# First front of a four-image hybrid network: two channel groups convolved on VectorE, first scan parts moved within the chip, edge count and scatters placed elsewhere

## The chip, the cores and the metric

The kernel runs on one core of one Trainium2 chip. The metric is the device time of one execution in microseconds; the time of the kernel before is the median of three runs. The profile is a further execution, recorded by the hardware profiler.

## What is computed

The input is four images of 32 x 32 pixels with 256 channels. Four layers follow: layer 0 (below), a bottleneck convolution with a residual, a graph attention over 1024 tokens with a mask made from a list of edges and a mixture of experts, and a second state-space layer with another mixture of experts. The first front belongs to layer 0:

```python
x = _layernorm(src, ln1_g, ln1_b)
x = x @ w_in + b_in                                   # 256 -> Dn = 512 channels
x = conv_general_dilated(x, conv_w, (1, 1), 'SAME', feature_group_count=Dn) + conv_b   # 3x3, depthwise
x = jax.nn.gelu(x)
proj = x @ w_x
dt_raw, Bm, Cm = jnp.split(proj, [R, R + N], axis=-1) # R = 16, N = 64
dt = jax.nn.softplus(dt_raw @ w_dt + dt_bias)
A = -jnp.exp(A_log)
def step(h, inp):
    xt, dtt, Bt, Ct = inp
    h = jnp.exp(dtt[:, :, None] * A) * h + (dtt * xt)[:, :, None] * Bt[:, None, :]
    return h, jnp.einsum('bdn,bn->bd', h, Ct)
```

The mask of the attention is `zeros((N, N)).at[src, dst].set(True)`.

## The kernel before, in words

**Scans and stages.** One generator, `scans` (line 366), runs all eight state-space scans (four images, layers 0 and 3) as 1280 scan units of 128 partitions x 1024 steps. It is the metronome of the kernel. For one unit, SP loads a decay tile (`load`, line 432: 512 KB, broadcast from the `dt` array in memory), ScalarE takes its exponential (`decay`), TensorE spreads a row of "parts" over the states (`first`: `ps_rep`), VectorE multiplies by B and runs `tensor_tensor_scan`, GpSimd multiplies by C (`h`), and TensorE sums over the states (`pair`: `ps_y`). Decay tiles have five buffers, `h` tiles five. `load` runs four units ahead.

Everything else is a *stage*: `front` (layer 0 up to the scan's inputs), `middle` (the end of layer 0 up to the scan inputs of layer 3), `last`. Stages are generators, too. `run` (562) advances the current stage between two half-units as long as the planned clocks of the engines (`Metered.COST`, a table of prices) are not ahead of VectorE's. So each engine's instructions stand in one fixed order, set by these prices at build time. Before the first unit can run, `need` (527) advances the first front until its first parts are ready: this is the prologue.

**The first front** (`front`, 711, with b = 0). The normalised image is transposed (`turned`), and for each of four groups of 128 channels (`DC` = 4) TensorE projects two halves of 512 pixels (`ps_in`), ScalarE writes them into a padded tile `pad` (34 x 34), ScalarE makes nine diagonal matrices of the taps (`diag`), and TensorE convolves: for each half nine fp32 matmuls of 128 x 512 with a diagonal matrix as weights (`ps_cv`). ScalarE applies the gelu and writes `u`. Then `ps_x` gives the 16 rows `dtr` and the B and C rows `bct`.

**The softplus items** (`steps`, 591). For each (group, half) TensorE makes `ps_dt`, ScalarE the pieces of the softplus, then dt (`sp_r`) and dt times u are formed, and the product is split into three bf16 parts (`parts`). In the first front the first two items are done by VectorE ahead of the others. SP stores dt (line 635) and parts (650) in memory; `chunk` (387) loads the B and C rows (401) and the parts, three loads of 32 partitions x 4 x 1024 (408), as the tile `S`, ahead of the units that use it; the pieces of S are addressed by j, 0 to 3, 32 channels each: the first 16 units use j = 0 and 1.

**The mask's work** is a third generator, `mask_work` (`setup`, 1846): tables for the scans (`scan_setup`, 323), then `mask_prepare` (1008): load the edges, transpose them (`ps_e`), make a linear index, count the edges of each row (`cnt`, `ps_c`), sort by eight rounds of `largest` (1089), switch on the count for rounds beyond 64 edges, and write the indices `where`. Then `scatter` (1112): 64 indirect DMAs by GpSimd that write zeros into a mask of 4 MB in memory, four switches for more columns, and one copy of the mask to bf16. `need` advances this generator once for each step of the front, `run` once for each unit.

**The vectors** (biases, gains, taps) are loaded by `load_vectors` (198) before all else: 27 small loads in two packs, each pack transposed by TensorE.

Of the kernel before, what the change touches and what calls it, by code (L numbers as in the profile page):

```python
# [16 lines left out]
P = 128  # L17
NB = 4
L = 1024
# [34 lines left out]
        ("L0_conv_conv_b", 4), ("L0_conv_dt_bias", 4), ("L0_conv_D_skip", 4), ("L0_conv_ln2_g", 4),  # L54
        ("L0_conv_ln2_b", 4), ("L1_conv_b1", 1), ("L1_conv_g1", 1), ("L1_conv_be1", 1),
        ("L1_conv_m1", 1), ("L1_conv_v1", 1), ("L1_conv_b2", 1), ("L1_conv_g2", 1),
        ("L1_conv_be2", 1), ("L1_conv_m2", 1), ("L1_conv_v2", 1), ("L2_attn_bq", 2),
        ("L2_attn_bk", 2), ("L2_attn_bv", 2), ("L3_attn_b_in", 8), ("L3_attn_b_conv", 4), ("L3_attn_b_dt", 4),
    ),
    (("L2_ffn_b1", 16), ("L3_ffn_b1", 32)),  # L60
)

# [70 lines left out]
class Hybrid:  # L133
    def __init__(self, ctx, tc, a, out):
        self.ctx, self.tc, self.nc, self.a = ctx, tc, tc.nc, a
        self.out = out.rearrange("b h w c -> (b h w) c")
        nc = self.nc
        self.const = const = ctx.enter_context(tc.tile_pool(name="const", bufs=1))
        self.dram = ctx.enter_context(tc.tile_pool(name="dram", bufs=1, space=DRAM))

        self.ident = const.tile([P, P], F32, name="ident")
        make_identity(nc, self.ident)
        self.identb = const.tile([P, P], BF16, name="identb")
        nc.vector.tensor_copy(self.identb, self.ident)

        order = const.tile([P, NEXP], I32, name="order")
        nc.gpsimd.iota(order, pattern=[[-1, NEXP]], base=NEXP, channel_multiplier=0)
        self.order = const.tile([P, NEXP], F32, name="orderf")
        nc.vector.tensor_copy(self.order, order)
        self.eps = {}  # L150
        for e in (1e-5, 1e-3):
            self.eps[e] = const.tile([P, 1], F32, name=f"eps{len(self.eps)}")
            nc.vector.memset(self.eps[e], e)

        self.x0 = const.tile([P, TB, C], F32, name="x0")
        nc.sync.dma_start(self.x0, self.image(a["x"].rearrange("b h w c -> (b h w) c"), 0))
        self.w_in0 = self.weight(const, "L0_conv_w_in", 2)
        for _ in self.norm(const, self.x0, TB, self.x0, "ln0"):
            pass

        self.blocks = const.tile([P, P], F32, name="blocks")
        make_block_diagonal(nc, self.blocks, 4)
        self.states = {0: 64, 3: 16}
        E = mybir.EngineType
        self.sides = (E.PE, E.DVE, E.Activation, E.SP)
        self.mem = {}
# [31 lines left out]
    def load_vectors(self):  # L198

        nc, a = self.nc, self.a  # L200
        self.vec = {}
        with self.tc.tile_pool(name="vstage", bufs=1) as sp, self.tc.tile_pool(
            name="vpsum", bufs=1, space=PSUM
        ) as pp:
            for n, pack in enumerate(VEC_PACKS):
                rows = sum(k for _, k in pack)
                stage = sp.tile([rows, P], F32, name=f"vstage{n}")
                r = 0
                for name, k in pack:
                    src = a[name]  # L210
                    if name == "L0_conv_conv_w":
                        src = src.rearrange("i j u (k p) -> (i j u k) p", p=P)
                    elif len(src.shape) == 2:
                        src = src.rearrange("e (k p) -> (e k) p", p=P)
                    else:
                        src = src.rearrange("(k p) -> k p", p=P)
                    nc.sync.dma_start(stage[r : r + k, :], src)
                    r += k
                ps = pp.tile([P, rows], F32, name=f"vps{n}")
                nc.tensor.transpose(ps, stage, self.ident[:rows, :rows])  # L220
                cols = self.const.tile([P, rows], F32, name=f"cols{n}")
                nc.vector.tensor_copy(cols, ps)
                r = 0
                for name, k in pack:
                    self.vec[name] = cols[:, r : r + k]
                    r += k
# [96 lines left out]
    def scan_setup(self, stage, name, n):  # L323
# [8 lines left out]
        flat = self.a[name].rearrange("(u g) n -> u (g n)", g=G)  # L332
        for k in range(0, units, P):
            m = min(P, units - k)
            raw = stage.tile([m, P], F32, name=f"Ar{k}_" + name)
            nc.sync.dma_start(raw, flat[k : k + m, :])
            turned = stage.tile([m, P], F32, name=f"At{k}_" + name)
# [23 lines left out]
        return cols, spread, collect  # L361
# [4 lines left out]
    def scans(self, mp, psum):  # L366
# [19 lines left out]

        def chunk(k):
# [6 lines left out]
            n = self.states[scan[0]]  # L394
            self.need(scan, d)
            if d == 0:
                bct = self.mem["bc", *scan]
                pair = []
                for t in range(2):
                    x = mp.tile([P, L], F32, tag=f"rows{t}", name=f"rows{t}", bufs=2)  # L400
                    nc.sync.dma_start(
                        x, bct[t * n : (t + 1) * n, :].unsqueeze(1).to_broadcast([n, P // n, L])
                    )
                    pair.append(x)
                rows[scan] = pair
            S = mp.tile([3 * 32, 4, L], BF16, tag="S", name="S", bufs=2)
            for s in range(3):
                nc.sync.dma_start(
                    S[32 * s : 32 * s + 32, :, :],
                    self.mem["parts", *scan, d][s].rearrange("(j p) t -> p j t", p=32),  # L410
                )
# [84 lines left out]

        for k in range(AHEAD):
            chunk(k)
        for k in range(4):
            load(k)  # L500
# [26 lines left out]
    def need(self, scan, d):  # L527

        late = False
        while ("parts", *scan, d) not in self.ready:  # L530
# [3 lines left out]
            for _ in range(SCATTERED if self.sorted else 1):  # L534
                next(self.mask_work, None)
        if late:

            self.clock.update(dict.fromkeys(self.clock, max(self.clock.values())))
# [23 lines left out]
    def run(self):  # L562
# [3 lines left out]
        self.alone = False  # L566
        nc, tc = self.nc, self.tc
        with tc.tile_pool(name="scan", bufs=1) as mp, tc.tile_pool(
            name="scps", bufs=1, space=PSUM
        ) as psum, tc.tile_pool(name="sdps", bufs=1, space=PSUM) as side, tc.manual_schedule():  # L570
            self.side_psum(side)
            self.mask_work, self.sorted = self.setup(), False
            clock = self.clock = dict.fromkeys(Metered.COST, 0.0)
            self.nc = Metered(nc, clock)
            for n, _ in enumerate(self.scans(mp, psum)):
                if n % 2:
                    next(self.mask_work, None)
                now = clock["vector"]
# [12 lines left out]
    def steps(self, fp, key, w, src, chunks, bias, u, between=None):  # L591
# [65 lines left out]
        if between is not None:  # L657
# [6 lines left out]
            yield from between  # L664
            for item in ahead:
                add(item, nc.vector)
            for item in ahead:
                split(item)
            for item in ahead:
                low(item, nc.vector)  # L670
            for item in ahead:
                store(item)
# [38 lines left out]
    def front(self, b):  # L711
# [3 lines left out]
        with tc.tile_pool(name=f"f{b}", bufs=1, side="right") as op:  # L715
# [4 lines left out]
            with tc.tile_pool(name=f"fa{b}", bufs=1, side="right") as fp:  # L720
# [8 lines left out]
                pads = [fp.tile([P, 34, 34], F32, name=f"pad{i}") for i in range(2)]  # L729
                for i in range(2):  # L730
                    nc.gpsimd.memset(pads[i], 0.0)
# [4 lines left out]
                yield from self.turned(x, TB, xT, (vec["L0_conv_ln1_g"], vec["L0_conv_ln1_b"]))  # L736
                got = {}

                def inward(item):
                    d, g, k = item  # L740
                    pad = pads[d % 2]
                    if g < 0:
# [10 lines left out]
                        )  # L753
                        if h == 0:
# [32 lines left out]
                items = []  # L787
                for d in range(DC):
                    items += [(d, -1, 0), (d, -1, 1)]
                    items += [(d, g, k) for g in range(2) for k in range(3)]  # L790
                yield from self.pipe(items, inward, cost=2.3)
            with tc.tile_pool(name=f"fb{b}", bufs=1, side="right") as fp:
# [215 lines left out]
    def mask_prepare(self):  # L1008
# [16 lines left out]
        with tc.tile_pool(name="mprep", bufs=1) as mp:  # L1025
# [15 lines left out]
            yield from [None] * 8  # L1041
# [6 lines left out]
            yield from [None] * 4  # L1048
            for a, rawf in enumerate(rawfs):
# [5 lines left out]
                yield  # L1055
# [21 lines left out]
            ps = self.early("ps_c")  # L1077
            nc.tensor.transpose(ps[:1, :P], cnt, self.ident)
            top = mp.tile([1, 1], F32, name="top")
            nc.vector.tensor_reduce(top, ps[:1, :P], AX.X, ALU.max)  # L1080
            more = mp.tile([1, len(SCATTERS)], F32, name="more")
            for i, (first, _) in enumerate(SCATTERS):
                nc.vector.tensor_scalar(more[:, i : i + 1], top, float(first), None, ALU.is_gt)
            nc.vector.tensor_copy(self.more, more)
            order = mp.tile([P, ne], F32, name="sorted")
            few = SCATTERS[0][1]
            nc.vector.memset(order[:, few:], 0.0)
# [9 lines left out]
            yield  # L1097
# [7 lines left out]
            yield  # L1105
# [3 lines left out]
        self.sorted = True  # L1109
# [66 lines left out]
    def attention(self, b, tb):  # L1176
        nc, tc, vec = self.nc, self.tc, self.vec
        with tc.tile_pool(name=f"at{b}", bufs=1, side="right") as op:
# [9 lines left out]
            with tc.tile_pool(name=f"aa{b}", bufs=1, side="right") as fp:  # L1188
# [25 lines left out]
                yield from self.large_scores(fp, qT, kT, large)  # L1214
                nc.sync.dma_start(maskT, self.mem[("maskT",)].rearrange("j p f -> p j f"))
# [630 lines left out]
    def setup(self):  # L1846
        with self.tc.tile_pool(name="prep", bufs=1) as st:
            yield
            self.tables = {}
            for scan, name, n in ((0, "L0_conv_A_log", 64), (3, "L3_attn_A_log", 16)):  # L1850
                self.tables[scan] = self.scan_setup(st, name, n)
                yield
        yield from self.mask_prepare()
# [35 lines left out]
def hybrid_kernel(tc, a, out):  # L1889
    with ExitStack() as ctx:  # L1890
        k = Hybrid(ctx, tc, a, out)
        k.load_vectors()
# [38 lines left out]
```

## Time and profile before

| | |
|---|---|
| median of three runs (lowest to highest) | 6504.83 us (6499.96 to 6507.34) |
| the profiled execution's own time | 6499.29 us |
| its span in the profile | 6497.3 us |
| mean granted TensorE clock | 0.831 |
| busy: TensorE, VectorE, ScalarE, GpSimd | 5253.9, 5119.6, 3415.4, 3646.8 us |
| first scan unit on VectorE starts at | 152.56 us |
| scan unit 256 starts its scan at | 1240.3 us |

How to read it: times of the timelines are in us from the span's start. A row shows its start, how long it took, the engine, the line, the operation with output and input tiles, and in brackets the idle time of the engine before it with what ended it. Nearly all operations carry the line of one helper (L124), so groups are told apart by the names of their tiles. In the rows of the stretches of time the columns are: stretch and its length, then the busy time (and number of instructions) of TensorE's matmuls, its weight loads, VectorE, ScalarE and GpSimd, then the granted TensorE clock, the busy share of the DMA engines and GB/s. A matmul of fp32 counts as two records.

### The profile page before, as it was taken

How to read it: one execution, taken by the hardware profiler on the slowest of the kernel's cores; microseconds unless marked ns; L12 is line 12 of the kernel's file. 1: busy time of each engine (PE TensorE's matmuls, PEld its weight loads, DVE VectorE, ACT ScalarE, POOL GpSimd, SP SyncE). 2: the span in 40 equal slices, each digit the busy share in tenths (PEclk: the TensorE clock that was granted, in tenths of full speed). 3: DMA queues.
4: the chain of work that ended last, by engine and by line, in shares of the span. 5: the costliest groups of instructions: out<-in, count | busy, mean ns of one | idle time of the engine just before them, and what ended most of it. 6: DMA issues, size and time to landing. Idle time of an engine off the chain costs nothing. (4 is left out here: it accounts for less than half of the span.)

```text
span 6497.3 us, 59722 instructions
## 1 busy us (share of the span) xinstructions
PE 5253.9 (81%) x20235; PEld 2124.1 (33%) x20320; DVE 5119.6 (79%) x4310; ACT 3415.4 (53%) x4095; POOL 3646.8 (56%) x1793
## 2 busy tenths in 40 slices
PE   6667868689797569979689679798699688978979
PEld 2022212222342022234145232252255222524656
DVE  3978988988898998889889988898899981258311
ACT  3346656355576335567568445577387354246311
POOL 2957677765557666555856665556756661055200
PEclk9577868689898569979789789898699689878989
DMA  2454554643355566335635664345544750156221
GB/s 101 145 163 159 180 163 160 198 150 124 119 174 170 180 169 164 113 128 184 195 132 176 195 159 135 112 146 178 182 164 163 196 148 15 46 147 166 68 67 34
DMA packets 348077, 936.58 MB, mean 144 GB/s; under 512 B 37140, under 2 KB 119648, under 8 KB 346144
## 3 DMA queue, kind: packets, MB, share of 16 engines
q1 hardware_dynamic: 345616, 930.35, 46.0%
q0 software_dynamic: 2128, 2.13, 0.2%
q8 instruction: 168, 2.75, 0.2%
q14 instruction: 165, 1.35, 0.1%
HBM read 842.59 MB, written 93.95 MB: 144 GB/s over the span
## 5 line engine op out<-in xcount | busy, mean ns | idle before, releaser
L124 POOL TENSOR_TENSOR h<-h,rows 128x1024 f32<-128x1024 f32 x1280 | 3033.0, 2372 | 1835.8 <-DVE h L124 1572.9
L124 DVE TENSOR_TENSOR_SCAN h<-dA,ps_rep 128x1024 f32<-128x1024 f32 x1280 | 2923.7, 2284 | 131.4 <-ACT dA L124 3.1
L124 DVE TENSOR_TENSOR ps_rep<-ps_rep,rows 128x1024 f32<-128x1024 f32 x1280 | 1551.7, 1212 | 188.5 <-PE ps_rep L124 183.9
L124 ACT ACTIVATE dA<-dA,A_L_conv_A_log 128x1024 f32<-128x1024 f32 x1024 | 1147.7, 1144 | 612.1 <-DMA dA<-dt 547.2
L124 PE MATMUL ps_rep<-S,spread_L_conv_A_log 96*128 96x512 bf16 x2048 | 763.2, 463 | 767.6 <-DVE h L124 716.2
L124 PE MATMUL ps_y<-h,collect_L_conv_A_log 128*32 128x512 f32 x4096 | 775.8, 767 | 61.5 <-POOL h L124 61.0
L124 PE MATMUL ps_h<-xTm,we 128*128 128x512 f32 x1536 | 714.2, 604 | 0.0
L124 PE MATMUL ps_e<-we,h_m 128*128 128x256 f32 x3072 | 700.4, 380 | 2.3 <-ACT h_m L124 2.3
L124 PEld LDWEIGHTS <-spread_L_conv_A_log 96*128 96x128 bf16 x2048 | 159.9, 103 | 1568.9 <-DVE h L124 1236.1
L124 ACT ACT_TABLE_LOAD x483 | 619.7, 1283 | 59.4 <-PE ps_h L124 44.1
L124 PEld LDWEIGHTS ps_e<-we,h_m 128*128 128x128 f32 x3072 | 579.4, 190 | 152.5 <-issue 61.1
L124 DVE SCALAR_TENSOR_TENSOR tb<-ps_e,cw,tb 128x256 f32<-128x256 f32 x512 | 219.9, 474 | 409.3 <-PE ps_e L124 409.2
L124 ACT ACTIVATE h_m<-ps_h,cols 128x512 f32<-128x512 f32 x384 | 260.2, 687 | 501.4 <-PE ps_h L124 498.9
L124 ACT ACTIVATE p<-ps_sc 128x512 f32<-128x512 f32 x432 | 234.5, 594 | 386.0 <-PE ps_sc L124 255.4
L124 PEld LDWEIGHTS ps_h<-xTm,we 128*128 128x128 f32 x1536 | 291.9, 193 | 331.7 <-issue 286.9
L124 ACT ACTIVATE dA<-dA,A_L_attn_A_log 128x1024 f32<-128x1024 f32 x256 | 290.6, 1146 | 200.0 <-DMA dA<-dt 172.3
L124 PE MATMUL ps_rep<-S,spread_L_attn_A_log 96*128 96x512 bf16 x512 | 185.8, 451 | 173.8 <-DVE h L124 161.0
L124 PE MATMUL ps_at<-p,v 128*32 128x512 f32 x1024 | 277.6, 623 | 4.8 <-ACT sums L124 4.6
L124 PE MATMUL ps_at<-p,ones 128*32 128x512 f32 x1024 | 277.6, 623 | 0.0
L124 PE MATMUL ps_sc<-qT,kT 32*128 32x512 f32 x864 | 262.9, 665 | 14.2 <-ACTq L1318 8.1
L124 PE MATMUL ps_cv<-pad,diag 128*128 128x512 f32 x576 | 262.3, 597 | 0.0
L124 PEld LDWEIGHTS ps_y<-h,collect_L_conv_A_log 128*32 128x32 f32 x4096 | 99.4, 119 | 436.9 <-issue 222.6
(327 smaller groups left out, 4865.4 us busy)
## 6 DMA issues: line engine op xcount, KB each, us to landing
dA<-dt SPq DMA_DIRECT2D x1280, 512.0 KB
we<-in_L_ffn_W_dram SPq DMA_DIRECT2D x64, 512.0 KB
parts<-parts SPq DMA_DIRECT2D x64, 384.0 KB
S<-parts SPq DMA_DIRECT2D x96, 256.0 KB
dt<-sp_r SPq DMA_DIRECT2D x64, 256.0 KB
y<-yo SPq DMA_DIRECT2D x128, 128.0 KB
y_back<-y SPq DMA_DIRECT2D x64, 256.0 KB
we<-in_L_ffn_w_dram SPq DMA_DIRECT2D x64, 256.0 KB
```

The source lines that it names most:

```text
L124: return got(*args, **kw)
```

## The change

1. Of the four channel groups of the first front, groups 2 and 3 (`BY_VECTOR`) are projected first, into two further pads, and convolved on VectorE: one multiplication and eight multiply-adds of 128 x 1024 straight into `u` (`beside`). Their gelu runs after that of groups 0 and 1 (`activate`). Groups 0 and 1 stay on TensorE. Fronts 1 to 3 are as before.
2. The first two items' parts go from their SBUF tiles to the tile `S` by 24 transfers of 32 partitions x 512 within the chip (`parts_direct`), instead of two stores and three loads: six for j = 0 on ScalarE's queue, 18 for the others on SP's. The B and C rows are loaded before dt is stored, the first two decay loads right behind that.
3. The vectors are loaded in three packs; the first only before the front, the other two within the mask's work, whose loads of edges and tables are all issued at its start.
4. In the mask's work, the sort's first eight rounds stand ahead of the count, and count and switch wait until the front is through its convolution (`reached`).
5. Scatters are issued only when GpSimd's planned clock is behind VectorE's. `need` runs the mask's work until it is sorted, and the attention runs what is left of it before it loads the mask.

The core of the diff:

```diff
@@ class Hybrid, __init__ @@
+        self.vec = {}
+        first = self.load_vectors(const, 0)
...
+            self.turn_vectors(0, first, pp.tile([P, P], F32, name="vps0"))
@@ scans @@
+        self.direct = mp.tile([3 * 32, 4, L], BF16, tag="S", name="S", bufs=2)
+
+        def parts_direct(js, queue):
+            for j in js:
+                for g, X in enumerate(self.first_parts):
+                    for s in range(3):
+                        queue.dma_start(
+                            self.direct[32 * s : 32 * s + 32, j, g * 512 : (g + 1) * 512],
+                            X[32 * j : 32 * j + 32, s, :],
+                        )
...
+            S = self.direct if k == 0 else mp.tile([3 * 32, 4, L], BF16, tag="S", name="S", bufs=2)
+            if k == 0:
+                parts_direct(range(1, 4), nc.sync)
+            elif d == 0:
+                load_rows(scan)
...
-        for k in range(4):
+        for k in range(2, 4):
             load(k)
@@ need @@
+        while not self.sorted:
+            next(self.mask_work)
@@ run @@
-                if n % 2:
+                now = clock["vector"]
+                if n % 2 and clock["gpsimd"] < now:
                     next(self.mask_work, None)
-                now = clock["vector"]
@@ steps @@
             yield from between
+            self.load_rows(key)
             for item in ahead:
                 add(item, nc.vector)
             for item in ahead:
                 split(item)
+            self.load(0)
+            self.load(1)
             for item in ahead:
                 low(item, nc.vector)
-            for item in ahead:
-                store(item)
+            self.first_parts = [got.pop(item)[1] for item in ahead]
+            self.parts_direct(range(1), nc.scalar)
+            self.ready.add(("parts", *key, 0))
@@ front @@
+                vector = () if b else BY_VECTOR
+                pads = [fp.tile([P, 34, 34], F32, name=f"pad{i}") for i in range(2 + len(vector))]
...
+                def beside(d, pad):
+                    to = u[:, d, :].rearrange("p (h w) -> p h w", w=32)
+                    for k in range(9):
+                        i, j = divmod(k, 3)
+                        window = pad[:, i : i + 32, j : j + 32]
+                        w = vec["L0_conv_conv_w"][:, k * DC + d : k * DC + d + 1]
+                        if k == 0:
+                            nc.vector.tensor_scalar(to, window, w, None, ALU.mult)
+                        else:
+                            nc.vector.scalar_tensor_tensor(to, window, w, to, ALU.mult, ALU.add)
...
-                items = []
+                items = [(d, -1, h) for d in vector for h in range(2)]
                 for d in range(DC):
-                    items += [(d, -1, 0), (d, -1, 1)]
-                    items += [(d, g, k) for g in range(2) for k in range(3)]
+                    if d not in vector:
+                        items += [(d, -1, 0), (d, -1, 1)]
+                        items += [(d, g, k) for g in range(2) for k in range(3)]
                 yield from self.pipe(items, inward, cost=2.3)
+                for d in vector:
+                    activate(d)
+                self.reached += 1
@@ mask_prepare @@
+            order = mp.tile([P, ne], F32, name="sorted")
+            few = SCATTERS[0][1]
+            nc.gpsimd.memset(order[:, few:], 0.0)
...
+            for r in range(0, few, 8):
+                largest(r)
+            while self.reached < 2:
+                yield
             ps = self.early("ps_c")
@@ attention @@
+                for _ in self.mask_work:
+                    pass
                 nc.sync.dma_start(maskT, self.mem[("maskT",)].rearrange("j p f -> p j f"))
@@ setup @@
+            masks = self.mask_prepare()
+            next(masks)
+            stages = [self.load_vectors(st, n) for n in (1, 2)]
...
+            while self.reached < 1:
+                yield
+            for t in tables:
+                next(t)
+            for n in (1, 2):
+                self.turn_vectors(n, stages[n - 1], self.early("vps"))
             yield
+            yield from masks
+        self.sorted = True
```

## The prediction

> **What bounds the kernel now.** I read the page first, then the chain of waits, then the stretches of time, then each engine's timeline up to 440 us. The chain of work that ended last is drawn only for the last sixth of the span, so it says nothing of the first front; the stage has to be read by itself. Three rows of the page give the beat of the middle (the columns: count | busy us, mean ns | idle before, and what ended it):
>
> ```profile
> L124 POOL TENSOR_TENSOR h<-h,rows 128x1024 f32<-128x1024 f32 x1280 | 3033.0, 2372 | 1835.8 <-DVE h L124 1572.9
> L124 DVE TENSOR_TENSOR_SCAN h<-dA,ps_rep 128x1024 f32<-128x1024 f32 x1280 | 2923.7, 2284 | 131.4 <-ACT dA L124 3.1
> L124 DVE TENSOR_TENSOR ps_rep<-ps_rep,rows 128x1024 f32<-128x1024 f32 x1280 | 1551.7, 1212 | 188.5 <-PE ps_rep L124 183.9
> ```
>
> A scan unit costs VectorE 2.284 + 1.212 us, and 3.54 from start to start; 1280 of them are 4531 of 6497 us, and VectorE hardly waits between them. Everything before the first unit (152.56 us) is a prologue in which VectorE scans nothing. TensorE's timeline shows what that prologue waits for:
>
> ```profile
> 31.13 15.62 PE L124 MATMUL ps_cv<-pad,diag 128*128 128x512 f32 x36
> 46.58 3.60 PE L124 MATMUL ps_in<-xT,w_L_conv_w_in 128*128 128x512 f32 x8
> ...
> 66.01 0.37 PE L124 MATMUL ps_c<-ident,cnt 128*1 128x128 f32 x1 [6.49 <-DVE cnt L124]
> 66.17 9.68 PE L124 MATMUL ps_cv<-pad,diag 128*128 128x512 f32 x18
> ...
> 113.56 7.04 PE L124 MATMUL ps_x<-u,w_L_conv_w_x 128*16 128x512 f32 x16
> ...
> 150.18 1.87 PE L124 MATMUL ps_rep<-S,spread_L_conv_A_log 96*128 96x512 bf16 x4 [16.86 <-DMA S<-parts]
> ```
>
> A convolved channel group is 15.6 us of TensorE and 3.6 of projection before it, four in a row to 113.6; the count of edges holds the queue for 6.5 us; and 16.9 us pass while the first parts go to memory and back. VectorE in the same time (its own timeline) is nearly free:
>
> ```profile
> 86.05 0.44 DVE L124 CAST where<-lin 128x544 int32<-128x544 f32 x1
> 127.34 0.69 DVE L124 SCALAR_TENSOR_TENSOR sp_e<-ps_dt,sp_e 128x512 f32<-128x512 f32 x1 [40.85 <-ACT sp_l L124]
> ...
> 151.22 1.23 DVE L124 TENSOR_TENSOR ps_rep<-ps_rep,rows 128x1024 f32<-128x1024 f32 x1 [12.77 <-PE ps_rep L124]
> 152.56 2.29 DVE L124 TENSOR_TENSOR_SCAN h<-dA,ps_rep 128x1024 f32<-128x1024 f32 x1
> ```
>
> SP's queue in that last gap: the order in which it must issue, each landing before the next dependent one:
>
> ```profile
> 133.97 0.32 SPq L810 DMA_DIRECT2D bc<-bct  x1
> 134.38 1.21 SPq L635 DMA_DIRECT2D dt<-sp_r  x2
> 137.75 1.11 SPq L650 DMA_DIRECT2D parts<-parts  x2
> 138.95 1.51 SPq L401 DMA_DIRECT2D rows<-bc  x2
> 141.60 1.29 SPq L408 DMA_DIRECT2D S<-parts  x3
> ```
>
> Behind the prologue, the stretches of time show a second loose place: 152 to 440 us holds 62 units, which at 3.54 would be 219.5; 67.5 us are lost there.
>
> ```profile
> 152.00:440.00 288.00, 178.84 (x421) 32.08 (x421) 238.09 (x186) 115.03 (x132) 220.30 (x131) 0.58 0.49 155
> 440.00:1240.00 800.00, 606.74 (x1870) 175.81 (x1868) 727.91 (x482) 492.61 (x641) 591.01 (x299) 0.76 0.52 173
> ```
>
> From VectorE's timeline the loss is 12 us at six softplus items of front 0 and their waits (units 0 to 45), 22 around GpSimd's four switches (units 46 to 50), 31.5 at the weights' preparation (units 55 to 60), 1.5 elsewhere.
>
> **What the Trainium skill says.** (1) "VectorE: DVE Perf Modes", perf-mode tier table: fp32 `tensor_tensor` runs at 1x, one-tensor operations on SBUF at 2x. The trace agrees: 1.29 us for 128x1088 with two tensors, 0.73 with one; scalar_tensor_tensor belongs to the first kind (1.26 us at 128x1024, the y_back row). (2) "TensorE: Matmul & The Clock Gate", What's actually happening: about 3.4 us of idleness halves the clock until TensorE has been busy as long. It agrees: after the 6.5 us wait, nine matmuls took 9.68 us instead of 7.8. (3) "SBUF — State Buffer", The DMA setup-cost knee: some 2 us are paid by each transfer whatever its size; here a 512 KB load waited on from issue (142.93) to use (151.2) had others queued ahead, so the trace gives no clean figure. (4) The same page, Who interferes with whom: a VectorE operation with two SBUF inputs contends only with a GpSimd operation that reads SBUF; GpSimd does none between 30 and 56 us before, nor, by the new order, during the new convolution.
>
> **The instructions' new order** was compared engine by engine. From unit 251 on all five queues hold the same instructions in the same order in both kernels; fronts 1 to 3 start at units 28, 94, 157 instead of 62, 125, 188. So everything behind unit 256 (1240.3 us before) is a shift, and the sum needs only two stages.
>
> **Stage 1, to the first scan.**
> - Tables: their loads are now behind four edge loads on SP (0.38+0.56+0.42+0.50 = 1.9 us; the other loads only change places), so the table copies start at 17.35+1.9 = 19.2. VectorE's table work took 17.35 to 27.78; with the two vector packs (0.26+0.21) and a wait for the projection now ahead of it on TensorE it ends at about 31.7. It hides the pad memsets and the first projections.
> - New on VectorE: each group 1 x 0.73 + 8 x (1.26+0.04) = 11.1 us. Group 2: 31.7 to 42.9; edge casts 1.1; group 3: 44.0 to 55.2. The strided window is not in the trace: lower end is this, upper end is 2x; I take this.
> - TensorE: new wait. The edge transposes stand ahead of the last projection of group 0 and wait for the casts, that is for group 2: idle from about 36 to 43.5; queued behind are all convolutions. Then 1.5 (transposes) + 1.8 + 15.6 + 3.6 + 15.6 = 81.7, and 2 for the halved clock: 83.7. Before: 113.6. Two groups' convolution (31.2) and the wait for cnt (6.5) are gone, this wait is new.
> - Sorting: from 55.2, copies 1.5, masks 8.3, eight rounds of 1.59 = 12.7: 77.8, hidden. The count then waits for the fronts; value_load and switch (4.5) and four small steps end at 95.5, 3 us ahead of VectorE's next work (sp_l at 98.4). If that cover goes, each us is on the path.
> - ScalarE: gelu 0.7, then two activations of 1.15 at the end, on the path: 86.9. TensorE's ps_x: 0.9+0.4+3.5 = 91.6; before 120.6. The step to the last bct copy is unchanged: 133.95-29.0 = 105.0.
> - Parts within the chip: bc store lands (2.5, estimate), rows issue 1.5, dt stores 1.2, now behind rows: the 1 MB of rows at about 250 GB/s and 0.5 MB of dt land at 114.6; first dA lands 3.4 later, decay 1.15: scan at 119.2. That is 14.2 after bct, before 18.6. The six pieces for j=0 on ACT's queue (0.3 to 0.85 each, before any decay is due) are hidden. The 18 pieces for j=1 to 3 on SP (0.38 each, 6.9) stand ahead of the loads of units 2 and 3: unit 2 about 1 late.
> - Moved at no cost: the 4 MB fill of the mask goes from 47.9 on SP's queue to about 20 (3.8 us of issue; behind it only u's stores, from 85 on, and no load that anybody waits for); without that cover it would cost its 3.8. The memset of the sorted tile goes to GpSimd (0.5), idle until the first scatter. The two part tiles stay taken until the 18 pieces have landed, near 125; the item that needs one of them again casts its parts after ten decays, near 150, so I price no wait. The two loops that run the mask's work to its end before the fronts' results or the mask are used issue nothing by then.
> Gain 152.56-119.2 = 33.4; bounds 25 (DMA issues at twice the price, a longer clock dip) and 40 (no dip, no late table).
>
> **Stage 2, units 0 to 256.** Same work, other places. The six items follow each other in units 3 to 20: per three units GpSimd 3 x 2.37 + 5.0 = 12.1 against 10.6, loss 12 to 17 (take 14). Preparation: same chain, 31.5. The four switches (4.4 us of GpSimd each) now fall in units 101 to 104, between convolutions where a unit takes 4.0 us: 4 x 6.8 - 16 = 11 behind, of which the five h buffers take about half: 6 instead of 22. Scatters: 4 before the first unit instead of 22, so 60 in units, at 1.17 each beside a 2.37 us product: 3.54 against 4.0; hidden, take 3, worst case below. 54.5 against 67.5: gain 13; bounds 0 and 30.
>
> **Sum.** Against the profiled execution: 6499.29-33.4-13 = 6453 (span 6451). That execution lies 5.5 us under the median of the runs shown, so I forecast 6458.
>
> **Rivals.**
> 1. Only half arrives (6478): the pieces' issue, the clock dip and late tables cost 10, and stage 2 gives only 3. For it: 24 small transfers and a queue never seen here. Against: SP's rows of 0.25 to 0.43 us. Chance 0.25 with the strided window at double price (group 3 then ends at 77 and the sort and count end 9 us after sp_l).
> 2. More (6438): table wait and dip absent, preparation less dear because fewer loads compete. 0.15.
> 3. Slower (6525): GpSimd becomes the bound in the fronts: 60 scatters of 1.17 us = 70 us on the path instead of 3. It decides once GpSimd's unit (2.37+1.17) plus its waits exceeds the 4.0 us of the front's unit. Against: 591 of 800 us busy in the stretch from 440 to 1240. 0.05.
> 4. The change does what it says by the order compared; that its gain is swallowed later would need another order behind unit 251, which there is not.
>
> **Chances.** Forecast 0.55 (own range 6446 to 6470), rivals 0.25, 0.15, 0.05. The range 6436 to 6484 leaves out rival 3 and the outer ends of 1 and 2. A measurement tells about 0.2% (13 us) from no change: faster 0.94, same 0.02, slower 0.04.
>
> **What would show it.** The first scan near 119 us; ps_cv twice 15.6 us, ending near 84, ahead of it one TensorE wait of some 7 us for rawf; two VectorE runs of 11 us on u; front 1's transposes near unit 28; unit 256 near 1194; afterwards a constant shift of about 46. A first scan after 128, or GpSimd over 90% busy in the fronts, would make it wrong.

## The result and the profile after

The changed kernel takes 6460.05 us (median of 5 runs, 6447.87 to 6467.65), beside 6504.34 us (5 runs, 6495.26 to 6507.34) for the kernel before on the same chip: a ratio of 0.993 with a 95% interval of 0.9917 to 0.9942. The forecast was 6458. How much of that nearness is earned is the main question below: the profiled execution took 6467.21 us (span 6465.4), and its trace is not 46 us ahead of before's at unit 256 but 29.

The costliest groups of the page show that the beat is what it was (count | busy us, mean ns | idle before, releaser):

```profile
L128 POOL TENSOR_TENSOR h<-h,rows 128x1024 f32<-128x1024 f32 x1280 | 3026.7, 2367 | 1816.9 <-DVE h L128 1567.0
L128 DVE TENSOR_TENSOR_SCAN h<-dA,ps_rep 128x1024 f32<-128x1024 f32 x1280 | 2923.0, 2284 | 142.8 <-ACT dA L128 12.8
L128 DVE TENSOR_TENSOR ps_rep<-ps_rep,rows 128x1024 f32<-128x1024 f32 x1280 | 1550.9, 1212 | 182.6 <-PE ps_rep L128 178.4
```

Scan and product cost VectorE 2.284 + 1.212 us in both kernels. TensorE's timeline of the prologue (start us, us, engine, line, operation, and in brackets the idle time before it and its releaser):

```profile
28.33 0.33 PE L128 MATMUL ps_A<-ident,At_L_attn_A_log 64*128 64x64 f32 x1 [6.75 <-DVE At_L_attn_A_log L128]
...
29.25 9.62 PE L128 MATMUL ps_in<-xT,w_L_conv_w_in 128*128 128x512 f32 x16
45.50 2.64 PE L128 MATMUL ps_e<-ident,rawf 128*128 128x128 f32 x10 [6.63 <-DVE rawf L128]
...
51.51 15.62 PE L128 MATMUL ps_cv<-pad,diag 128*128 128x512 f32 x36
66.96 3.60 PE L128 MATMUL ps_in<-xT,w_L_conv_w_in 128*128 128x512 f32 x8
70.39 15.62 PE L128 MATMUL ps_cv<-pad,diag 128*128 128x512 f32 x36
...
102.65 5.33 PE L128 MATMUL ps_x<-u,w_L_conv_w_x 128*128 128x512 f32 x8 [3.48 <-ACT bct L128]
117.85 1.13 PE L128 MATMUL ps_rep<-S,spread_L_conv_A_log 96*128 96x512 bf16 x2 [9.87 <-DMA S<-parts]
125.92 1.09 PE L128 MATMUL ps_rep<-S,spread_L_conv_A_log 96*128 96x512 bf16 x2 [6.94 <-DMA S<-parts]
```

Two convolutions instead of four, ending at 86.0; the wait for the edge casts is there as foretold (6.63 us). Not foretold is the last line: TensorE waits a second time, 6.94 us, for the pieces of unit 1. VectorE's timeline:

```profile
33.79 0.75 DVE L128 TENSOR_SCALAR u<-pad,cols 128x1024 f32<-128x1024 f32 x1 [1.96 <-ACT pad L128]
34.58 10.53 DVE L128 SCALAR_TENSOR_TENSOR u<-pad,cols,u 128x1024 f32<-128x1024 f32 x8
45.02 1.01 DVE L128 CAST rawf<-raw 128x512 f32<-128x512 int32 x4
...
46.74 10.53 DVE L128 SCALAR_TENSOR_TENSOR u<-pad,cols,u 128x1024 f32<-128x1024 f32 x8
...
123.66 2.29 DVE L128 TENSOR_TENSOR_SCAN h<-dA,ps_rep 128x1024 f32<-128x1024 f32 x1 [3.41 <-ACT dA L128]
127.05 1.23 DVE L128 TENSOR_TENSOR ps_rep<-ps_rep,rows 128x1024 f32<-128x1024 f32 x1 [1.11 <-PE ps_rep L128]
128.39 2.29 DVE L128 TENSOR_TENSOR_SCAN h<-dA,ps_rep 128x1024 f32<-128x1024 f32 x1
...
137.49 2.29 DVE L128 TENSOR_TENSOR_SCAN h<-dA,ps_rep 128x1024 f32<-128x1024 f32 x1 [5.69 <-ACT dA L128]
141.84 0.69 DVE L128 SCALAR_TENSOR_TENSOR sp_e<-ps_dt,sp_e 128x512 f32<-128x512 f32 x1 [2.07 <-ACT sp_l L128]
...
143.78 2.29 DVE L128 TENSOR_TENSOR_SCAN h<-dA,ps_rep 128x1024 f32<-128x1024 f32 x1
```

The first scan starts at 123.66 (before 152.56), but units 1 and 2 follow after 4.7 and 9.1 us instead of 3.54. Of TensorE's wait for unit 1, VectorE feels only 1.11 us; it loses most, 5.69 us, to the late decay tile of unit 2. SP's queue shows what stands ahead of that tile's load:

```profile
111.24 1.23 SPq L404 DMA_DIRECT2D rows<-bc  x2
115.20 0.81 SPq L667 DMA_DIRECT2D dt<-sp_r  x2
118.95 1.18 SPq L468 DMA_DIRECT2D dA<-dt  x2
120.22 12.17 SPq L416 DMA_DIRECT2D S<-parts  x18
132.43 17.69 SPq L468 DMA_DIRECT2D dA<-dt  x8
```

Eighteen pieces take 12.17 us of issue, 0.68 each, and the load of unit 2 goes out behind them at 132.43. The stretches of time (us, then busy time and count of each engine, granted clock, DMA share, GB/s) show the first 62 units and the rest up to unit 256:

```profile
123.00:409.00 286.00, 210.64 (x629) 67.87 (x630) 239.04 (x185) 156.73 (x205) 222.34 (x132) 0.73 0.51 160
409.00:1211.00 802.00, 547.72 (x1662) 138.87 (x1660) 735.77 (x482) 450.81 (x568) 608.75 (x316) 0.67 0.55 173
```

62 units still take 286 us, 66 above the beat. By starts of units in the traces, in us:

| unit | before | after | ahead by |
|---|---|---|---|
| 0 | 152.6 | 123.7 | 28.9 |
| 3 | 163.7 | 143.8 | 19.9 |
| 20 | 227.6 | 216.9 | 10.7 |
| 28 | 256.1 | 275.9 | -19.8 |
| 62 | 439.5 | 409.0 | 30.5 |
| 256 | 1240.3 | 1211.0 | 29.3 |
| span's end | 6497.3 | 6465.4 | 31.9 |

The preparation lies at units 20 to 28 after and at 55 to 60 before, hence the swing between.

### The profile page after: what moved, and what is told of

It is laid out like the page before. It is cut to its first block, busy times and chain, and to the rows that moved or that the text cites. A ratio compares the mean times of both kernels' runs of the same rounds, so it can differ in the third digit from the quotient of the medians.

```text
span 6465.4 us, 59678 instructions
## 1 busy us (share of the span) xinstructions
PE 5210.1 (81%) x20249; PEld 2107.8 (33%) x20249; DVE 5153.1 (80%) x4328; ACT 3408.1 (53%) x4075; POOL 3648.4 (56%) x1796
## 5 line engine op out<-in xcount | busy, mean ns | idle before, releaser
L128 DVE TENSOR_TENSOR_SCAN h<-dA,ps_rep 128x1024 f32<-128x1024 f32 x1280 | 2923.0, 2284 | 142.8 <-ACT dA L128 12.8
L128 PE MATMUL ps_y<-h,collect_L_conv_A_log 128*32 128x512 f32 x4096 | 739.5, 773 | 14.6 <-POOL h L128 14.6
L128 POOL TENSOR_TENSOR sp_l<-sp_l,sp_e 128x512 f32<-128x512 f32 x62 | 78.4, 1265 | 272.4 <-DVE sp_e L128 250.5
L128 PE MATMUL ps_cv<-pad,diag 128*128 128x512 f32 x504 | 230.9, 599 | 0.0
```

Of the source, the lines that this page charges most:

```text
L128: return got(*args, **kw)
```

## Experiments

The theory at the outset was the prediction's own: the time is won in the prologue, by the convolution and the order there, and the pacing only moves work. The rivals: that the pacing is a main part; that the prologue's gain is given back in the first units. Each kernel is the changed one with one edit. Times are medians; "unit 256" is its start in the kernel's one trace. Each group was run beside the kernel before (medians of 6504.34 to 6509.46, with the result's own). Differences are taken from the changed kernel's 6460.05 and its first trace; a second median of it, in another group, is 6457.95, and the ratios' intervals are 12 to 20 us wide. So a few us of a median are not clear of noise.

**The convolution back on TensorE.**

```
-BY_VECTOR = (2, 3)
+BY_VECTOR = ()
```

> The changed kernel with all four groups convolved on TensorE again; everything else of the change stays, and behind unit 0 all queues hold the same order. Theory A (each part acts by the time it takes on the prologue's path): TensorE gets two more convolutions and no wait for the edge casts; its convolution ends near 106 instead of 86, the two late activations (2.2 us) go, so the first scan comes 15 to 20 us later (139 to 144 us instead of 123.7), and the run takes 15 to 20 us longer than the changed kernel. Theory B (the gain comes from the mask's work and the denser fronts, the convolution is hidden by other waits): first scan within 5 us of the changed kernel, total the same.

6484.63 us, ratio 0.9974 (0.9965 to 0.9983): 24.6 slower than the changed kernel. Convolutions end at 108.3 instead of 86.0, the first scan is at 146.4 (22.7 later) and unit 256 at 1227.5 (16.5 later). So the VectorE convolution is worth some 20 us, as the theory had it, though first scan and median went a few us beyond its upper ends (144 and 20). Of the parts undone here it moves the first scan most.

**The first parts by way of memory.** Every item is stored, and unit 0 loads S with three loads from memory like all others.

```
-            if k == 0:
-                parts_direct(range(1, 4), nc.sync)
...
-            self.first_parts = [got.pop(item)[1] for item in ahead]
-            self.parts_direct(range(1), nc.scalar)
-            self.ready.add(("parts", *key, 0))
+            for item in ahead:
+                store(item)
```

> The changed kernel with the first parts stored to memory and loaded as tile S again (two stores, three loads), the rest as changed. Theory A (the 24 small transfers cost their issue, 0.68 us each on SP in the changed kernel's profile, and the loads of units 2 and 3 wait behind 18 of them): the first scan comes later (near 131 instead of 123.7), but units 2 and 3 then follow without their waits, so unit 3 is at 140 to 144 as in the changed kernel (143.8); total within 5 us. Theory B (staying within the chip is worth the round trip through memory): everything from the first scan on is 7 us later or more.

6463.27 us, ratio 0.9939 (0.9925 to 0.9952). The first scan is 11.5 us later (135.2), unit 3 only 2.6 (146.4 against 143.8), unit 20 at 217.1 against 216.9, unit 256 at 1211.5 against 1211.0. The move within the chip wins its time at unit 0 and loses it by unit 20: it bought nothing in this form (3.2 us of the median, within the noise).

**The pacing of the scatters taken out.**

```
-                if n % 2 and clock["gpsimd"] < now:
+                if n % 2:
```

> The changed kernel without the pacing of scatters (one per unit from unit 0 on whatever GpSimd's planned clock). Fronts 1 to 3 then start at units 71, 134, 197 instead of 28, 94, 157, and the order differs from the changed kernel's up to unit 467. Theory A (pacing only chooses which units the scatters share): the first scan is unchanged, unit 256 within 8 us, total between 0 and 12 us slower, the part that is lost lying at the four switches that again meet the softplus items. Theory B (pacing is a main part of the gain): 20 us or more slower.

6485.55 us, ratio 0.9971 (0.9960 to 0.9983): 25.5 slower, so here the theory fell and the rival held. Fronts 1 to 3 start at units 71, 134 and 197 instead of 28, 94 and 157. Unit 46 is even reached early (306.9 against 342.0), and units 46 to 94 then take 250.2 us against 210.1. These 40 us are not the loss itself: the preparation, which costs the changed kernel 33 us ahead of unit 46, falls into them here, while less of front 1 does. At unit 94 the run is 5.0 behind (557.1), at unit 256 18.7 (1229.7), and at unit 467, from where the order is the same again, 17.6 (2161.2). VectorE's waits from unit 46 to 94 show where much of it arises (for what, on whom, us, times, longest), first without pacing:

```profile
DVE row_L_conv_b_out L128 <- PE ps_b L128: 15.8, 1, 15.8
DVE ps_rep L128 <- PE ps_rep L128: 14.3, 6, 4.9
DVE sp_x L128 <- ACT parts L128: 13.7, 2, 7.8
DVE ln_st L128 <- DMA x<-in_x_dram: 7.7, 1, 7.7
```

and in the changed kernel:

```profile
DVE ps_rep L128 <- PE ps_rep L128: 10.1, 2, 5.5
DVE sp_e L128 <- ACT sp_l L128: 3.8, 1, 3.8
```

Over all of units 3 to 256, so wherever the side work stands, VectorE waits 24.8 us for `parts` without pacing and 11.2 with it, and 15.8 against 3.7 for the preparation's `ps_b`: 25.7 us more for these two, and the long ones lie in the stretch shown. Without pacing the last items, the switches and the preparation meet in those units: the last of front 0's six items comes to GpSimd at 390 us, in the changed kernel at 202. GpSimd's timeline before they meet:

```profile
306.57 1.00 POOL L128 DMA_INDIRECT mask_dram<-zero,where  x1 [0.17 <-issue]
307.60 2.35 POOL L128 TENSOR_TENSOR h<-h,rows 128x1024 f32<-128x1024 f32 x1
310.12 1.01 POOL L128 DMA_INDIRECT mask_dram<-zero,where  x1 [0.17 <-issue]
311.15 2.36 POOL L128 TENSOR_TENSOR h<-h,rows 128x1024 f32<-128x1024 f32 x1
```

One scatter to each unit makes 2.36 + 1.00 + 0.17 = 3.53 us, all of a beat, so that the program's planner finds little room on GpSimd for the items until the scatters are through. (That the planner's account puts them off is argued from the code; the times of the items are shown.) GpSimd is full as in rival 3, but in the kernel that lacks the pacing.

**The count of edges not held back.**

```
-            while self.reached < 2:
-                yield
```

> The changed kernel with the count of edges ahead of the convolution on TensorE again (no wait for the front's end; the sort still ahead of the count). Theory A: TensorE waits for the count until VectorE has made it, near 67 us, before it starts a convolution at 51.5 now; first scan 15 to 19 us later (139 to 143), some of it given back because 20 scatters instead of 4 precede unit 0; total 10 to 19 us slower. Theory B (the count's place is indifferent once the convolution is shorter): within 5 us.

6472.21 us, ratio 0.9953 (0.9940 to 0.9967): 12.2 slower. The count stands in TensorE's queue ahead of a convolution again; convolutions end at 104.8, the first scan is at 142.8. Of those 19.1 us, 8.1 are left at unit 256 (1219.1). Here 20 scatters instead of 4 stand ahead of the first unit, so 16 fewer among the units. That this gives the other 11 us back isn't shown: leaving out all of them, in a run below, gains 11.6.

**The casts ahead of group 2.** VectorE casts the edges before its first convolved group, so that TensorE has them in time.

```
             for t in tables:
                 next(t)
+            next(masks)
...
                 rawfs.append(rawf)
+            yield
             yield from [None] * 3
```

> The changed kernel with the edge casts moved ahead of the tables on VectorE (nothing else moves), so that TensorE does not wait for them between the projections. Theory A (that wait of 6.6 us is on the path and halves the clock behind it, some 3 us more): the wait is gone, convolution ends near 77 instead of 86, first scan 114 to 117 instead of 123.7, total 6 to 9 us faster. Theory B (the sort and count on VectorE take its place): first scan at 121 or later, total the same.

6453.25 us, ratio 0.9915 (0.9902 to 0.9927): 6.8 faster than the changed kernel. Its TensorE timeline:

```profile
29.35 9.68 PE L128 MATMUL ps_in<-xT,w_L_conv_w_in 128*128 128x512 f32 x16
38.86 1.53 PE L128 MATMUL ps_e<-ident,rawf 128*128 128x128 f32 x10
```

The wait of 6.63 us is gone, and the ten transposes take 1.53 us instead of 2.64. Convolutions end 9.3 earlier (76.6), the first scan is 7.8 earlier, unit 256 is 8.3 earlier. So the new wait that the prediction priced was on the path, and nothing up to unit 256 took it back; the 6.8 us of the median alone would not be clear of noise.

**Another order at the start.** dt is stored before the rows load, and the twelve pieces for j = 2 and 3, which by the kernel's list of units none before unit 32 uses, go behind the loads of units 2 and 3.

```
-            self.load_rows(key)
...
+            self.load_rows(key)
             self.load(0)
...
-                parts_direct(range(1, 4), nc.sync)
+                parts_direct(range(1, 2), nc.sync)
...
         for k in range(2, 4):
             load(k)
+        parts_direct(range(2, 4), nc.sync)
```

> The changed kernel with another order on SP ahead of unit 0: dt stores before the B and C rows, and of the 18 pieces of S only the 6 for j=1 ahead of the loads of units 2 and 3, the other 12 behind them. Theory A (the order of SP's queue is what units 0 to 3 wait for): dA of unit 0 lands 3 to 5 us earlier, first scan near 120, units 2 and 3 without their waits: unit 3 at 132 to 135 instead of 143.8; total 7 to 11 us faster. Theory B (the transfers' rate is what they wait for): unit 3 within 3 us of 143.8, total the same.

6450.78 us, ratio 0.9914 (0.9901 to 0.9927): 9.3 faster than the changed kernel. SP's queue:

```profile
106.96 1.20 SPq L668 DMA_DIRECT2D dt<-sp_r  x2
109.25 1.23 SPq L404 DMA_DIRECT2D rows<-bc  x2
113.29 1.22 SPq L468 DMA_DIRECT2D dA<-dt  x2
115.08 3.78 SPq L416 DMA_DIRECT2D S<-parts  x6
118.91 1.60 SPq L468 DMA_DIRECT2D dA<-dt  x2
120.57 8.45 SPq L416 DMA_DIRECT2D S<-parts  x12
```

The loads of units 2 and 3 go out at 118.91 instead of 132.43. The first scan is 4.3 earlier and units 0 to 3 take 11.2 us instead of 20.1; unit 256 starts 11.9 earlier (1199.1). The 4.3 us belong to dt's place: its store goes out at 106.96 instead of 115.20, and the first decay loads at 113.29 instead of 118.95, so loading the rows first, as the change does, held unit 0 back. The other 8.9 us are the cost of the pieces' place in the queue. The second experiment agrees: by way of memory, with the rows still first, units 0 to 3 take 11.1 us.

**Both together.**

> Both edits together, casts early and start order. If both waits lie one behind the other on the path, their gains add: unit 3 at 122 to 127, total 14 to 19 us faster than the changed kernel. If one hides the other, no more than the better of the two.

6442.64 us (6441.9 to 6456.9), ratio 0.9907 (0.9893 to 0.9921): 17.4 less, where the two alone give 6.8 + 9.3 = 16.1. Unit 256 starts at 1194.0, 17.0 earlier. This version beats both kernels.

**Without the scatters.** The scatters are left out and the mask is filled with zeros, so edges are not masked; the order of all else is kept.

```
-            nc.gpsimd.memset(neg, NEG)
+            nc.gpsimd.memset(neg, 0.0)
...
+            self.clock["gpsimd"] += 1.0
+            return
             nc.gpsimd.indirect_dma_start(
```

> The changed kernel without the 64 scatters (their planned cost is kept, so that all other instructions keep their order) and with the mask filled with zeros, so that no edge is masked: that part of the computation is left out. Theory A (60 scatters within the units are hidden beside the convolving fronts): unit 256 0 to 6 us earlier, total 0 to 6 us faster. Theory B (GpSimd's 1.17 us per scatter lie partly on the path): unit 256 earlier by 15 us or more.

6458.11 us, ratio 0.9923 (0.9910 to 0.9935). Unit 256 starts 11.6 us earlier (1199.4), the median is 1.9 less. It lies between the theories at unit 256 and gives nothing at the end; what the scatters cost isn't settled beyond 0 to 12 us.

**The preparation apart from its loads, and a second trace of the changed kernel.**

```
                 yield 0.5
+            for _ in range(8):
+                yield 0.5
             for part in parts:
                 for _ in part:
                     pass
-                yield 3.0
+                for _ in range(4):
+                    yield 3.0
```

> The weights' preparation is begun about four units after its loads instead of at once, and its four parts stand further apart; fronts 1 to 3 start some 7 units later, and the order is after's own behind unit 232. Theory A (the 34 us lost in units 21 to 28 are waits of VectorE's in-order queue for weights just loaded, and for TensorE, with the scan's own loads stuck behind them on the same DMA queue): 10 to 18 us less at unit 256, 8 to 18 less in the median. Theory B (the stall is the chain of the preparation's own work, VectorE to TensorE and back, whenever it starts): 0 to 5 less.

6461.56 us, ratio 0.9923 (0.9909 to 0.9937); unit 256 at 1209.7. VectorE's timeline in it:

```profile
243.13 0.42 DVE L128 TENSOR_TENSOR row_L_conv_b_out<-row_L_conv_b_out,ps_b 128x256 f32<-128x256 f32 x1 [5.85 <-PE ps_b L128]
250.51 1.22 DVE L128 TENSOR_TENSOR w_L_conv_w_out<-w_L_conv_w_out,ps_m 128x1024 f32<-128x1024 f32 x1 [3.87 <-PE ps_m L128]
258.22 0.56 DVE L128 TENSOR_TENSOR w<-ps_w,blocks 128x384 f32<-128x384 f32 x1 [1.74 <-PE ps_w L128]
```

and the same lines in the changed kernel:

```profile
227.48 0.42 DVE L128 TENSOR_TENSOR row_L_conv_b_out<-row_L_conv_b_out,ps_b 128x256 f32<-128x256 f32 x1 [3.66 <-PE ps_b L128]
232.70 1.22 DVE L128 TENSOR_TENSOR w_L_conv_w_out<-w_L_conv_w_out,ps_m 128x1024 f32<-128x1024 f32 x1 [3.61 <-PE ps_m L128]
237.96 0.56 DVE L128 TENSOR_TENSOR w<-ps_w,blocks 128x384 f32<-128x384 f32 x1 [1.73 <-PE ps_w L128]
```

The same waits come back, later: units 20 to 32 take 76.8 us against 75.5. Waiting for fresh loads is not what the preparation costs, and my theory of it fell; the lines fit its own chain, VectorE to TensorE and back, with the scan queued behind. On top of the version with both edits it gave nothing either:

> Casts early and the start order together, with the preparation spaced as well. Theory A (the gains add): as much below 6443 as the spaced preparation alone is below the changed kernel; with 10 to 18 that is 6425 to 6433. Theory B (what is gained at the front is waited away later): 6440 to 6445.

6444.12 us, ratio 0.9894 (0.9879 to 0.9909), beside 6442.64 without it. The changed kernel by itself, again:

> The changed kernel unchanged, beside the next two. Theory A (its executions scatter by some 15 us around a median of 6460, and the gain in the trace at unit 256 is 29 of 1240): a profile of its own has its first scan at 123 to 125, unit 256 at 1209 to 1213, and a median of 6456 to 6468. Theory B (the first profile was a slow one from the start): unit 256 at or under 1200 and a median under 6455.

6457.95 us, ratio 0.9921 (0.9907 to 0.9934), span 6454.7: first scan at 123.4 and unit 256 at 1210.3, within 1 us of the first trace. From there to the end the two traces take 5254.4 and 5244.4 us, 10 us apart for the same instructions.

**The kernel before, a second trace.**

> The kernel before, unchanged, for a second trace of it. By the medians the changed kernel is 44 to 51 us shorter, by two traces each only 29 to 30 at unit 256, with the same order of instructions behind it. Theory A (the first trace of before was an execution whose first 256 units were short): unit 256 at 1246 or later, and from there to the end 5243 to 5253 as in the changed kernel's traces and those of its variants. Theory B (the front is what the first trace shows, and the rest of the kernel takes longer in before for a reason that the order doesn't show): unit 256 at 1238 to 1243, and 5255 to 5265 from there to the end.

6505.85 us, ratio 1.0 (0.9992 to 1.0008), span 6511.3. VectorE in it:

```profile
154.93 1.23 DVE L124 TENSOR_TENSOR ps_rep<-ps_rep,rows 128x1024 f32<-128x1024 f32 x1 [12.46 <-PE ps_rep L124]
156.26 2.29 DVE L124 TENSOR_TENSOR_SCAN h<-dA,ps_rep 128x1024 f32<-128x1024 f32 x1
```

The first scan is 3.7 us later than in the first trace, unit 256 6.8 later (1247.1), and from there to the end it takes 5264.2 us (first trace 5257.0). So both theories hold in half: the first trace had a short front, and what lies behind unit 256 is also long.

## Why the prediction came out as it did

**The sum.** By two traces each, unit 256 starts at 1243.7 before and 1210.7 after: 33 us of the 46 that were forecast. From there to the end the means are 5260.6 and 5249.4: 11 us that the prediction put at nought, because the order is the same. 33 + 11 = 44, which is the difference of the medians. The forecast of 6458 is thus near 6460 partly by luck, because two errors cancel. Two of the prediction's own signs did not come: unit 256 near 1194 (1211.0 and 1210.3), and a constant shift of 46 behind it. Whether those 11 us are an effect of the change stays open: the ten variants' traces, all with the changed kernel's order behind unit 467 at the latest, show 5243.6 to 5260.1 in the same place, which the first trace of before lies within and the second exceeds by 4. The 11 us stand in VectorE's waits for TensorE's `ps_rep` there, 141.6 and 146.5 us before, 138.9 and 127.0 after. But the same wait also makes up the difference between the two traces of the changed kernel, so it need not be the change that lengthens it; what does isn't shown.

**Stage 1, right in mechanism, 4.5 us short** (33.4 forecast, 28.9 in the first pair of traces, 30.9 by two traces each; the first scan was forecast at 119.2 and came at 123.7 and 123.4).
- Group on VectorE: 0.75 + 10.53 = 11.3 us, 11.1 forecast. The eight multiply-adds on the window of 32 by 32 in rows of 34 take 10.53 us, 1.32 each from start to start; the price from contiguous operations held, and the doubled price of rival 1 did not come. (Of one-tensor operations the page that the prediction names gives 2x to `tensor_copy` and `tensor_scalar`, not to all; the convolution's first operation is a `tensor_scalar`.)
- VectorE's first group began at 33.8, not 31.7 (it waited for ScalarE's pad, and that for a projection, which on TensorE stood behind the tables, the wait of 6.75 us in the first row of its timeline above). That moved the casts and so the end of the convolutions to 86.0 instead of 83.7. The clock dip, priced at 2, was there: ten transposes took 2.64 us after the wait and 1.53 without it, the projection 3.60 instead of 1.98, 2.7 together; the clock granted from 45 to 52 us was 0.55, from 52 to 67 us 1.00. It agrees with the Trainium skill, "TensorE: Matmul & The Clock Gate", What's actually happening, by which about 3.4 us of idleness halve the clock.
- From there to the last bct copy it took 1.3 more than forecast. TensorE's last eight `ps_x` took 5.33 us at a granted clock of 0.69, in the kernel before 3.70 at 1.00, though both stood behind a wait of 3.48 us; why the clock fell only once isn't shown. From the bct copy to the scan it took 0.9 more (15.1, 14.2 forecast); the estimate of 2.5 for the bc store fits, since the rows' load went out 2.6 after it (108.62, 111.24). The count stayed covered: VectorE ended it at 98.1 and its next work began at 100.4.

**The step that failed: "the 18 pieces for j=1 to 3 on SP (0.38 each, 6.9)", unit 2 "about 1 late".** The pieces took 0.68 us each, 12.2 in all. And the term was set against unit 2 alone, as though its load had slack; in fact VectorE waits 1.1 us for unit 1's pieces, 5.7 for the decay tile of unit 2, whose load stands behind all eighteen, and 2.1 ahead of unit 3 for ScalarE, and units 0 to 3 took 20.1 us where before took 11.1. That is 9 us instead of 1. The start-order run shows it, since it gets 8.9 of them back by moving only issues on SP.

**Stage 2, nearly right behind unit 3:** 1067.2 us from there to unit 256 against 1076.6, a gain of 9.4 where 13 was forecast (by the second traces 1066.9 against 1079.7, 12.8). Counted from unit 0, the 9 us above take nearly all of it away: 1087.3 against 1087.7. Items lost 12.9 over the beat (14 forecast), the preparation 33 over units 20 to 32 (31.5), the switches 9.4 (three units took 20.0 us; 6 forecast). "60 scatters hidden, take 3" is bounded by 0 to 12.

**What I hadn't asked: which part of the change pays.** The prediction took the earlier fronts from the order and gave stage 2 a gain of 13 for the lot; the run without pacing is 25.5 slower. The undone parts sum to 24.6 + 3.2 + 25.5 + 12.2 = 65.5, more than the 44 they make together: they are not additive. A likely reason, not tested, is that each undone edit leaves the others at work in another order. The third part of the change, the vectors in three packs with the early loads, was not undone by itself, so its share is open.

**Rivals.** Rival 1's mechanism (the pieces' issue above all) came true without its doubled window; rival 2's missing wait can be had (casts early) but was not in this kernel; rival 3 didn't come in the changed kernel (without scatters it gains 0 to 12 us, not 67), while a GpSimd filled by scatters is what the run without pacing shows; rival 4 did not come: the lead of 29.3 at unit 256 is 31.9 at the end (36.8 and 56.6 in the second traces).

## What to carry to other kernels

A move within the chip that becomes many small transfers is paid in the issue of the queue it stands on: count the loads behind it, and send the pieces only when their unit is next (twelve of the eighteen here were not needed before unit 32). Side work spread evenly over an engine (one scatter to each unit) can fill exactly the slack that other work on it needs; each undone alone, pacing it (25.5 us) was worth as much here as taking half the convolution off TensorE (24.6). When a stage's gain is read from one trace, take a second trace of both kernels before the last 10 us are explained.

## What the hardware showed unexpectedly

- An SBUF to SBUF piece costs 0.68 us of issue on SP's queue (18 in 12.17) and 0.64 on ScalarE's (6 in 3.82), well above the 0.25 to 0.43 of single loads from which I had estimated; the loads of rows and decay tiles around them take 0.6 (1.23 and 1.18 for two), so a queue's issues are not all of one price.
- fp32 scalar_tensor_tensor on a strided window (32 rows of 32 in a pitch of 34) takes 1.285 us for 128x1024, against 1.260 contiguous (`y_back`, the median in before). That fp32 `tensor_tensor` runs at 1x is in the Trainium skill, "VectorE: DVE Perf Modes", perf-mode tier table; the runs show `scalar_tensor_tensor` about as slow as the `tensor_tensor` product (1.21 to 1.23 us), and that this stride costs 2%.
- The same instructions in the same order differ by 10 us of 5250 between two traced executions of the changed kernel, and by 7 us between two of the kernel before.
